# Reading lists ahead and reordering the rounds of a fused attention and expert kernel

## The chip, the core and the metric

The kernel runs on one core of a Trainium2 chip. The metric is device time in microseconds (us). The engines are TensorE (PE, with its weight loads as PEld), VectorE (DVE), ScalarE (ACT), GpSimd (POOL), and SyncE (SP), which issues most transfers. Each engine works through its own instructions in order, and waits between engines are semaphores.

## The reference

Eight batches of 512 tokens with 256 features go through one block:

```python
x = x + tanh(g_xattn[0]) * xattn(layernorm(x), ctx, ctx, mask)   # 16 heads of 16, softmax
x = x + tanh(g_ffn[0]) * ffn(layernorm(x))

def ffn(x):                                   # x: 4096 tokens x 256
    logits = x @ router_w + router_b          # 8 experts
    probs = softmax(logits)
    top_w, top_idx = top_k(probs, 2)
    comb = sum(top_w[..., None] * one_hot(top_idx, 8), axis=1)
    for e in range(8):
        h = gelu(x @ expert_up[e].T)          # 1024 wide
        output += comb[:, e] * (h @ expert_down[e].T)
    return output
```

All of it is float32. The mask leaves no more than 128 neighbouring keys here, and the kernel's near path reads only these; of the experts it computes only the two that a token has chosen.

## The kernel before

**Rounds.** `attend_near` runs rounds b = -1 to 7. A round has four groups g of three steps n, and a place in it is written (g,n). In round b the kernel computes the attention of batch b and the score maxima of batch b+1. `weights_T` (L1051 on) makes `w_ps` on TensorE and the exponentials `n_pT` on ScalarE; `weigh` makes `n_av` on TensorE and `raw`, `inv`, `n_o`, `oT` on VectorE; `find_tops` makes `t_ps` on TensorE and `tops` on VectorE; `lower_tops` makes `top_ps` and `ql`.

`between(old, new, next_)` lays further steps into the places of a round. They belong to the batch before (old = b-1), to the batch that is attended two rounds later (new = b+2) and to the one after that (next_ = b+3):

- old: `project_out` (`proj_ps`, and `x` on VectorE), `keep_x` (`out<-x` on SyncE), the statistics (`look`: `st_f_a`, `mv_f_a`), `settle` (a chain of 12 small VectorE operations that makes `rstd_end` and `shift`), the scalings `xn_f` on ScalarE (`scale`, L275), `keep_rows` (`rows<-xn_f` on SyncE), two turns (`xnT_ps_f`, then `x2T` on ScalarE) and the router's `logits` (`route_ps`, `lgT`).
- new: `keys_values` (`kv_ps`), the scalings `xn_a`, two turns (`xnT_ps_a`, `n_xnT`), `keys_T` (`k_ps`, `k`), `keys_less` (`km`), the queries (`q_ps`, `q`) and `add_bias` (GpSimd adds `bo` to `x`, 128x1024).
- next_: its statistics, settled together with those of old.

One round later, `route` (L330) transposes the logits (`lg_ps`), adds the bias (`lg`) and chooses two experts a token with some fifteen small VectorE operations and one exponential on ScalarE (`pr`). `place` (L363) counts with two pairs of matmuls (`place_ps`) at which line of its expert's list a token stands; ScalarE copies `counts`, and GpSimd works out `place_i`. Four `enter` steps a batch (L398), of two indirect transfers each, write the entries into a table in memory. At three points (in rounds 4 and 7 and in the tail) a plan divides what the table holds into groups of 256 rows, each with its expert.

**Groups.** A group s of rows goes through `list_rows(s)` (SyncE reads its list, `listed<-table`), `load(s)` (`up` and `down` of its expert, 1 MB each, SyncE, three buffers each), `fetch(s)` (GpSimd gathers `xg<-rows`), `turn` (`x_ps`, `xT`), `ups` (`h_ps` on TensorE, `hT` by Gelu on ScalarE), `fetch_y` (`y<-out`), and `downs` (`o_ps`, `y`, and GpSimd's `out<-y`). Groups 0 to 3 lie in rounds 4 to 7 by the table `amid`; groups 4 to 31 make up the tail. There `compute(s)` issues the steps of a group, with the list of group s+4 and the load of group s+2 at its end, and after each step takes one from a queue that holds what is left of the last two batches.

**What orders the work.** The program order is what the loops write. Instructions under `keep_in_program_order` (the first of a batch's scalings, first statistics, `settle`, the matmuls of scores and weights, and others) keep their place on their engine; the scheduler may move others. PSUM has one buffer for `n_av` and `o_ps` (`ps_o`), two for `bank` tiles (`ps_g`: `kv_ps`, `lg_ps`, `xnT_ps`, `k_ps`, `q_ps`, `top_ps`, `place_ps`, `proj_ps`, `route_ps`) and five for `t_ps`, `w_ps` and `x_ps` (`ps_s`). So a `bank` tile that waits holds up those behind it, and TensorE with them.

Of the kernel before, what the change touches and what calls it, by code (L numbers as in the profile page):

```python
# [23 lines left out]
E, FF = 8, 1024  # L24
# [44 lines left out]
def flamingo_layer(ctx: ExitStack, tc: tile.TileContext, a: dict, out: bass.AP):  # L69
# [190 lines left out]
    def shared(p2, small, bank):  # L260
        def layernorms(jobs, pin=False, measured=None):


            said, looks, settle_all = measured or measure(small, [job[:2] for job in jobs], pin)
            settle = lambda pin=False: settle_all(pin)

            def own(k):
                b, which, dst = jobs[k]

                def scale(ts):  # L270
                    if ts[0] == 0:
                        said[k] = p2.tile([P, QT, D], F32, tag="xn", name=f"xn_{which}_{b}")
                    for t in ts:
                        at = k * QT + t
                        ins = nc.scalar.activation(  # L275
                            said[k][:, t, :], xs[b][:, t, :], AF.Identity,
                            bias=said["shift"][:, at : at + 1], scale=said["rstd"][:, at : at + 1],
                        )
                        if t == ts[0] and pin:
                            tc.keep_in_program_order(ins)  # L280

                def turn(c):
                    ps = bank(f"xnT_ps_{which}_{b}_{c}")
                    for t in range(QT):
                        nc.tensor.transpose(ps[:, t * P : (t + 1) * P], said[k][:, t, c * P : (c + 1) * P], ident)
                    nc.scalar.copy((dst() if callable(dst) else dst)[:, c, :], ps)  # L286

                return (
                    lambda: said[k], [lambda ts=ts: scale(ts) for ts in ((0, 1), (2, 3))],
                    [lambda c=c: turn(c) for c in range(DC)],  # L290
                )

            return looks, settle, [own(k) for k in range(len(jobs))]
# [7 lines left out]
        def finish(b):  # L301
# [28 lines left out]
            def route():  # L330
                ps = bank(f"lg_ps{b}")[:, :P]
                nc.tensor.transpose(ps, said["lgT"], ident)
                lg = t3("lg")
                nc.vector.tensor_tensor(
                    lg, ps.rearrange("p (t e) -> p t e", t=QT)[:, :, :E], over_t(rb), ALU.add
                )
                mx = t2("mx")
                nc.vector.tensor_reduce(mx, lg, AX.X, ALU.max)
                nc.vector.tensor_tensor(lg, lg, over_e(mx), ALU.subtract)
                pr = t3("pr")  # L340
                nc.scalar.activation(pr, lg, AF.Exp)
                sm = t2("sm")
                nc.vector.tensor_reduce(sm, pr, AX.X, ALU.add)
                rs = t2("rs")
                nc.vector.reciprocal(rs, sm)
                nc.vector.tensor_tensor(pr, pr, over_e(rs), ALU.mult)
                top = t3("top")
                idx = t3("idx", U32)
                for t in range(QT):
                    nc.vector.max(top[:, t, :], pr[:, t, :])  # L350
                    nc.vector.max_index(idx[:, t, :], top[:, t, :], pr[:, t, :])
                ix = t3("ix")
                nc.vector.tensor_copy(ix, idx)
                picks = small.tile([P, QT, 2, E], F32, tag="picks", name=f"picks{b}", bufs=2)
                nc.vector.tensor_tensor(
                    picks, iota.unsqueeze(1).unsqueeze(1).to_broadcast([P, QT, 2, E]),
                    ix[:, :, :2].unsqueeze(3).to_broadcast([P, QT, 2, E]), ALU.is_equal,
                )
                both = t3("both")
                nc.vector.tensor_tensor(both, picks[:, :, 0, :], picks[:, :, 1, :], ALU.add)  # L360
                said["top"], said["picks"], said["both"] = top, picks, both
# [40 lines left out]
                    )  # L402

            places = [place] + [lambda t=t: enter(t) for t in range(b * QT, (b + 1) * QT)]
            return x2T, keep_x, keep_rows, logits, route, places

        return layernorms, finish

# [220 lines left out]
    def experts(pool, seen, half_bank, bank, row_bank):  # L629
# [281 lines left out]
        def downs(s):  # L911
            return [lambda h=h: go_down(s, h) for h in range(halves(s))]

        def compute(s, end, first):

            steps = [lambda: fetch(s + 2)] if s + 2 < end else []
            if s > first:
                steps.append(lambda: fetch_y(s - 1))
            up = ups(s)
            last = downs(s - 1) if s > first else []  # L920
            if s + 1 < end and s >= ALONE:
                turned_next = turns(s + 1)
                for step in up:
                    steps += [step, *turned_next[:1]]
                    turned_next = turned_next[1:]
                steps += turned_next + last
            elif s + 1 < end:
                steps += up + [lambda: turn(s + 1)] + last
            else:

                steps += up[:2] + last + up[2:]
            if s + 4 < end:
                steps.append(lambda: list_rows(s + 4))
            if s + 2 < end:
                steps.append(lambda: load(s + 2))
            if s + 1 == end:
                steps += [lambda: fetch_y(s), *downs(s)]
            return steps
# [29 lines left out]
    def attend_near(att):  # L968
# [143 lines left out]
        def between(old, new, next_):  # L1112
# [7 lines left out]

            jobs = []
            if old is not None:
                x2T, keep_x, keep_rows, logits, route, place = finish(old)
                jobs.append((old, "f", x2T))
            if next_ is not None:
                xnT[next_] = None
# [3 lines left out]
            if new is not None:  # L1130
# [4 lines left out]
                if new == 1:  # L1135
                    put(1, 1, *turns)
                    put(2, 1, keys_T)
                    put(3, 1, queries[0])
                    put(3, 2, queries[1], keys_less)
                else:  # L1140
                    put(1, 1, *turns, keys_T)
                    put(3, 0, keys_less)
                    put(2, 0, queries[0])
                    put(2, 1, queries[1])
# [4 lines left out]
                if new > 1:  # L1149
                    put(3, 0, bias)  # L1150
            if next_ is not None:
                put(*((2, 2) if old is None else (0, 2)), looks[-1])
            if old is not None:
                rows_f, scales, turns = normal[old, "f"]
                put(0, 1, lambda: project_out(old, (0, 1)))
                put(1, 0, lambda: project_out(old, (2, 3)), keep_x)
                put(1, 1, looks[0])
            if jobs:
                put(*((3, 1) if old is None else (1, 2)), settle)
            if old is not None:  # L1160
                put(2, 0, *scales)
                put(2, 2, lambda: keep_rows(rows_f()))
                put(3, 0, *turns)
                put(3, 1, logits)
                place, *enter = place
                counts = [count for count, end in zip(plans, PARTS) if old + 1 == end]
                later.append((route, place, enter, counts))
            return plan


        def begin():
# [19 lines left out]
            (7, 1): downs(2) + [lambda: load(4), lambda: turn_rows(3)],  # L1191
            (7, 2): [lambda: fetch_y(3)] + ups(3),
            (7, 3): [lambda: list_rows(5), lambda: fetch(5)] + downs(3)
            + [lambda: load(5), lambda: turn_rows(4), lambda: list_rows(6), lambda: list_rows(7)],
        }
        DONE = 4


        xnT, later = {}, deque()
# [4 lines left out]
        for b in range(-1, B):  # L1204
# [10 lines left out]
            if b == 0:  # L1215
                plan[0, 0] += looks
                plan[0, 1].insert(0, settle)
            for route, place, enter, counts in behind_route:
                plan[0, 2].append(route)
                plan[1, 2].append(place)  # L1220
                if counts:
                    plan[1, 2] += enter + counts
                else:
                    for where, step in zip(((1, 2), (2, 0), (2, 1), (2, 2)), enter):
                        plan[where].append(step)
            for g in range(4):
                c, i = g // 2, g % 2
# [17 lines left out]
        weigh(*behind)  # L1245
        rest = [step for steps in between(B - 1, None, None).values() for step in steps]
        wait = lambda: None
        (route, place, enter, _), (route_last, last, enter_last, counts) = later
        mixed = [step for pair in zip(rest, [route, place, *enter] + [wait] * len(rest)) for step in pair]
        spread = [step for one in enter_last for step in (one, wait, wait)]  # L1250
        queue = deque([*mixed, route_last, last, *spread, *counts])
        for s in range(DONE, MAIN):
            for step in compute(s, MAIN, DONE):
                step()
                if queue:
                    queue.popleft()()
                    if not queue:
                        assert s < ALONE
                        heads.close()
                        open_wide()  # L1260
# [3 lines left out]
    def attend_anywhere(att):  # L1264
# [141 lines left out]
            )  # L1406

        def end(b):
            x2T, keep_x, keep_rows, logits, route, place = finish(b)
            (look,), settle, ((normal, scales, turns),) = layernorms([(b, "f", x2T)])  # L1410
            return [keep_x, look, settle, *scales, lambda: keep_rows(normal()), *turns, logits, route, *place]

        def scores(b, h, t):
            q, kT, _ = qkv[b]
# [176 lines left out]
```

## Time and profile before

| | |
|---|---|
| median of 15 runs | 814.06 us (811.56 to 816.89) |
| profiled execution | 814.41 us |
| its span, first to last instruction | 812.6 us |
| mean granted TensorE clock | 0.971 |
| rounds -1 and 0, with the preparation | 0 to 69.8 us |
| rounds 1, 2, 3, 4 (from one `kv_ps` to the next) | 31.0, 39.1, 41.0, 38.2 us |
| rounds 5 to 7 | 219 to about 350 us |
| tail | about 350 us to the end |

The profile's page gives each engine's busy time and its share of the span, and the span in 40 slices of 20.3 us, in which a digit is the busy share in tenths. PEclk is the clock that the throttle granted to TensorE, in tenths of full speed. A timeline gives a start, a duration, the engine, the line, the operation, output and inputs, and in brackets the idle time of the engine just before, with what ended it. "remote" there means that no instruction of the profile was found to end the wait. Busy times by stretches give, behind the stretch and its length, a busy time and a count for each engine.

### The profile page before, as it was taken

What the parts mean: (1) busy time and instruction counts of PE and PEld (TensorE: products, weight loads), DVE (VectorE), ACT (ScalarE), POOL (GpSimd) and SP (SyncE); (2) the same over time, 40 slices, a digit from 0 to 9 for tenths busy, and PEclk for the clock granted to TensorE, in tenths of its full rate; (3) what the DMA queues carried; (4) which work ended last, traced back from release to release, by engine and by line L of the source; (5) the groups of instructions that cost most, each with busy time, mean ns of one, the idle gap of its engine ahead of it and who ended that gap; (6) DMA issues with size and microseconds to landing.
All of it is one profiled execution on the core that took longest, in us unless ns stands there. A gap on an engine that the chain in (4) does not pass through costs nothing.

```text
span 812.6 us, 11155 instructions
## 1 busy us (share of the span) xinstructions
PE 753.8 (93%) x3898; PEld 542.1 (67%) x3898; DVE 409.1 (50%) x1315; ACT 254.8 (31%) x487; POOL 313.2 (39%) x420
## 2 busy tenths in 40 slices
PE   8999988878989989998899999999999999999992
PEld 3444443434465656767688888888788788878872
DVE  8887895858673564633262352525343433523300
ACT  4563735354644434243312111111211211121110
POOL 2021115152636251546573534444443443344331
PEclk9998997989999999999999999999999999999997
DMA  5700211000473330143738566665754754654310
GB/s 163 264 7 8 78 33 56 27 30 27 153 284 110 108 115 20 53 146 91 262 107 319 187 211 218 191 237 180 248 168 151 239 182 151 200 199 177 99 52 25
DMA packets 82728, 113.32 MB, mean 139 GB/s; under 512 B 16605, under 2 KB 67552, under 8 KB 82656
## 3 DMA queue, kind: packets, MB, share of 16 engines
q1 hardware_dynamic: 70000, 85.16, 31.4%
q0 software_dynamic: 11840, 26.76, 10.0%
q8 instruction: 35, 0.57, 0.3%
q10 hardware_dynamic: 816, 0.53, 0.2%
q14 instruction: 37, 0.30, 0.1%
HBM read 92.66 MB, written 20.28 MB: 139 GB/s over the span
## 4 chain that ended last, share of the span: by engine, by line
PE 44%; DMA 15%; issue 14%; DVE 12%; POOL 8%; ACT 4%; another core or an unknown queue 1%; POOLq 0%; DVEq 0%; SPq 0%; ACTq 0%
PE o_ps L892 13%; PE h_ps L874 11%; DMA out<-y,listed 8%; DMA y<-out,listed 5%; PE w_ps L1058 5%; PE t_ps L1028 3%; PE n_av L1076 3%; DVE tops L1033 3%; DVE xT L863 2%; PE kv_ps L539 2%; POOL out L898 2%; PE proj_ps L1097 2%; POOL y L826 2%; DMA xg<-rows,listed 2%; PE top_ps L1046 1%
## 5 line engine op out<-in xcount | busy, mean ns | idle before, releaser
L892 PE MATMUL o_ps<-down,hT 128*128 128x256 f32 x1088 | 243.3, 381 | 4.7 <-DVE y L895 4.7
L874 PE MATMUL h_ps<-xT,up 128*128 128x256 f32 (+1 forms) x1024 | 242.9, 393 | 3.2 <-DVE xT L851 2.3
L892 PEld LDWEIGHTS o_ps<-down,hT 128*128 128x128 f32 x1088 | 206.1, 191 | 40.8 <-DVE y L895 6.3
L874 PEld LDWEIGHTS h_ps<-xT,up 128*128 128x128 f32 x1024 | 193.2, 190 | 46.0 <-issue 4.9
L863 DVE STREAM_TRANSPOSE xT<-xg 32x128 f32<-32x128 f32 (+1 forms) x368 | 115.6, 314 | 181.4 <-DMA xg<-rows,listed 176.6
L878 ACT ACTIVATE hT<-h_ps 128x512 f32<-128x512 f32 (+1 forms) x144 | 81.9, 573 | 346.2 <-PE h_ps L874 306.1
L898 POOL DMA_INDIRECT out<-y,listed x68 | 68.5, 1008 | 144.2 <-DVE y L895 125.7
L826 POOL DMA_INDIRECT y<-out,listed x68 | 65.0, 956 | 81.6 <-DMA out<-y,listed 56.7
L1033 DVE TENSOR_REDUCE tops<-t_ps 128x4 f32<-128x512 f32 x128 | 79.4, 682 | 21.3 <-PE t_ps L1028 16.6
L1063 ACT ACTIVATE n_pT<-w_ps 128x512 f32<-128x512 f32 x128 | 67.8, 597 | 49.4 <-PE w_ps L1058 47.0
L826 POOL DMA_INDIRECT xg<-rows,listed x68 | 66.5, 978 | 37.8 <-issue 18.9
L398 POOL DMA_INDIRECT table<-entries,place_i x64 | 63.2, 988 | 24.4 <-issue 16.1
L895 DVE SCALAR_TENSOR_TENSOR y<-o_ps,listed,y 128x256 f32<-128x256 f32 x68 | 31.1, 481 | 73.1 <-PE o_ps L892 51.0
L1058 PE MATMUL w_ps<-ql,km 32*128 32x512 f32 x256 | 53.8, 691 | 1.8 <-DVE tops L1033 1.4
L1010 POOL TENSOR_TENSOR x<-x,bo 128x1024 f32<-128x1024 f32 x8 | 18.8, 2354 | 72.4 <-DVE bo L1009 42.4
L1082 DVE STREAM_TRANSPOSE raw<-n_av 128x512 f32<-128x512 f32 x32 | 22.8, 712 | 46.7 <-PE n_av L1076 20.6
L1028 PE MATMUL t_ps<-k,q 32*128 32x256 f32 x512 | 43.8, 408 | 1.2 <-ACT n_pT L1063 0.7
L1028 PEld LDWEIGHTS t_ps<-k,q 32*128 32x128 f32 x512 | 26.8, 184 | 22.4 <-issue 9.7
L1076 PE MATMUL n_av<-n_pT,nv 128*32 128x512 f32 x256 | 38.4, 675 | 1.1 <-DVE xT L851 1.1
L570 PE MATMUL q_ps<-n_xnT,wqT 128*128 128x512 f32 x64 | 31.4, 615 | 0.9 <-ACT n_xnT L286 0.6
L1097 PE MATMUL proj_ps<-woT,oT 128*128 128x256 f32 x128 | 31.5, 388 | 0.0
L391 POOL TENSOR_SCALAR entries<-top,tg 128x8 f32<-128x8 f32 x8 | 2.6, 325 | 70.3 <-DVE top L350 70.2
(220 smaller groups left out, 552.7 us busy)
## 6 DMA issues: line engine op xcount, KB each, us to landing
up<-in_upT SPq DMA_DIRECT2D x32, 1024.0 KB
down<-in_downT SPq DMA_DIRECT2D x32, 1024.0 KB
out<-x SPq DMA_DIRECT2D x8, 512.0 KB
rows<-xn_f SPq DMA_DIRECT2D x8, 512.0 KB
x<-in_x SPq DMA_DIRECT2D x7, 512.0 KB
table<-none SPq DMA_DIRECT2D x1, 2400.0 KB
xg<-rows,listed POOLq DMA_INDIRECT x68
y<-out,listed POOLq DMA_INDIRECT x68
```

Of the source, the lines that this page charges most:

```text
L398: nc.gpsimd.indirect_dma_start(out=table_parts[2 * t + i][:, :], out_offset=bass.IndirectOffsetOnAxis(ap=place_i[:, t, i : i + 1], axis=0) ...
L826: ins = nc.gpsimd.indirect_dma_start(out=dst, out_offset=None, in_=src[: seen[JOBS[s][0]], :], in_offset=bass.IndirectOffsetOnAxis(ap=list ...
L863: nc.vector.transpose(dst[32 * g : 32 * g + 32, i], src[32 * i : 32 * i + 32, g])
L874: nc.tensor.matmul(ps[:, i, :], lhsT=up[:, dc, (f + i) * P : (f + i + 1) * P], rhs=xT[:, dc, :], start=(dc == 0), stop=(dc == DC - 1),)
L878: nc.scalar.activation(made[s][:, f : f + m, :], ps, AF.Gelu)
L892: nc.tensor.matmul(ps, lhsT=hT[:, f, h * P : (h + 1) * P], rhs=down[:, f, :], start=(f == 0), stop=(f == FC - 1))
L898: ins = nc.gpsimd.indirect_dma_start(out=out_parts[h][:, :], out_offset=bass.IndirectOffsetOnAxis(ap=listed[:, n, h, 0:1], axis=0), in_=y[ ...
L1028: ins = nc.tensor.matmul(ps[j][:, u], lhsT=q[rows_j, c, t * P : (t + 1) * P], rhs=k[rows_j, c], start=True, stop=True)
L1033: nc.vector.tensor_reduce(top[:, 2 * tp : 2 * tp + 2, :].rearrange("p t (i x) -> p t i x", i=2)[:, :, :, 32 * j], ps[j], AX.X, ALU.max,)
L1058: ins = nc.tensor.matmul(ps[j], lhsT=km[rows_j, c, i, :], rhs=lowered[b, c][rows_j, i, :], start=True, stop=True)
L1063: nc.scalar.activation(pT[:, j, :], ps[j], AF.Exp)
L1076: ins = nc.tensor.matmul(av[32 * j : 32 * j + 32, :], lhsT=made_of(b)[3][:, 8 * c + 2 * j + r, :], rhs=pT[:, j, :], start=True, stop=True,)
```

## The change

1. **Lists.** In round 7, SyncE reads the lists of groups 6 to 16 together, behind the load of group 5 (before: 6 and 7 there, and the others in the tail, each behind the group four before it).
2. **Scalings.** All `xn_f` and `xn_a` scalings are pinned to their place in the program order, not only the first of a batch.
3. **Choice.** `route` is divided: `lg_ps` and `lg` go from (0,2) to (0,0), the choice of experts (`choose`, from `mx` to `both`) from (0,2) to (1,2), behind the statistics and `settle`, with its first operation pinned. In the rounds with a plan (4 and 7) both stay at (0,2).
4. **Place.** `place` goes from (1,2) to (2,2), and the table writes of a batch from (1,2), (2,0), (2,1), (2,2) to (2,2), (3,0), (3,1), (3,2), in the rounds without a plan.
5. **Keys.** `keys_T` goes from (1,1) to (1,2).
6. **The first round.** In rounds that have no old batch, the last statistics go from (2,2) to (1,2) and `settle` from (3,1) to (2,0).
7. **Queue of the tail.** The route and choice of a batch are one step, and the steps of the last but one are paired in the same order as before.

```diff
-                        if t == ts[0] and pin:
+                        if pin:
                             tc.keep_in_program_order(ins)
...
+            def choose():
+                lg = said["lg"]
                 mx = t2("mx")
-                nc.vector.tensor_reduce(mx, lg, AX.X, ALU.max)
+                tc.keep_in_program_order(nc.vector.tensor_reduce(mx, lg, AX.X, ALU.max))
...
-            if s + 4 < end:
+            if listed <= s + 4 < end:
                 steps.append(lambda: list_rows(s + 4))
...
-                    put(1, 1, *turns, keys_T)
+                    put(1, 1, *turns)
+                    put(1, 2, keys_T)
...
-                put(*((2, 2) if old is None else (0, 2)), looks[-1])
+                put(*((1, 2) if old is None else (0, 2)), looks[-1])
...
-                put(*((3, 1) if old is None else (1, 2)), settle)
+                put(*((2, 0) if old is None else (1, 2)), settle)
...
-            + [lambda: load(5), lambda: turn_rows(4), lambda: list_rows(6), lambda: list_rows(7)],
+            + [lambda: load(5), lambda: turn_rows(4), lambda: [list_rows(s) for s in range(6, LISTED)]],
         }
         DONE = 4
+        LISTED = SIZES[0] + SIZES[1]
...
-            for route, place, enter, counts in behind_route:
-                plan[0, 2].append(route)
-                plan[1, 2].append(place)
+            for route, choose, place, enter, counts in behind_route:
                 if counts:
-                    plan[1, 2] += enter + counts
+                    plan[0, 2] += [route, choose]
+                    plan[1, 2] += [place, *enter, *counts]
                 else:
-                    for where, step in zip(((1, 2), (2, 0), (2, 1), (2, 2)), enter):
+                    plan[0, 0].append(route)
+                    plan[1, 2].append(choose)
+                    for where, step in zip(((2, 2), (2, 2), (3, 0), (3, 1), (3, 2)), (place, *enter)):
                         plan[where].append(step)
...
-            for step in compute(s, MAIN, DONE):
+            for step in compute(s, MAIN, DONE, LISTED):
```

`LISTED` is 17: the first two plans have 5 and 12 groups.

More of the change, by code (lines that the diff above doesn't have):

```diff
@@ L332, in route @@
                 nc.tensor.transpose(ps, said["lgT"], ident)
[L333 removed]
+                said["lg"] = t3("lg")
                 nc.vector.tensor_tensor(
[L335 removed]
+                    said["lg"], ps.rearrange("p (t e) -> p t e", t=QT)[:, :, :E], over_t(rb), ALU.add
                 )
+            def choose():
+                lg = said["lg"]
                 mx = t2("mx")
[L338 removed]
+                tc.keep_in_program_order(nc.vector.tensor_reduce(mx, lg, AX.X, ALU.max))
                 nc.vector.tensor_tensor(lg, lg, over_e(mx), ALU.subtract)
@@ L404, in finish @@
             places = [place] + [lambda t=t: enter(t) for t in range(b * QT, (b + 1) * QT)]
-            return x2T, keep_x, keep_rows, logits, route, places
+            return x2T, keep_x, keep_rows, logits, route, choose, places
         return layernorms, finish
@@ L912, in downs, with compute @@
             return [lambda h=h: go_down(s, h) for h in range(halves(s))]
-        def compute(s, end, first):
+        def compute(s, end, first, listed=0):
             steps = [lambda: fetch(s + 2)] if s + 2 < end else []
@@ L1122, in between @@
             if old is not None:
-                x2T, keep_x, keep_rows, logits, route, place = finish(old)
+                x2T, keep_x, keep_rows, logits, route, choose, place = finish(old)
                 jobs.append((old, "f", x2T))
@@ L1166, in between @@
                 counts = [count for count, end in zip(plans, PARTS) if old + 1 == end]
-                later.append((route, place, enter, counts))
+                later.append((route, choose, place, enter, counts))
             return plan
@@ L1247, in attend_near, with choice @@
         wait = lambda: None
-        (route, place, enter, _), (route_last, last, enter_last, counts) = later
-        mixed = [step for pair in zip(rest, [route, place, *enter] + [wait] * len(rest)) for step in pair]
+        (route, choose, place, enter, _), (route_last, choose_last, last, enter_last, counts) = later
+        def choice(route, choose):
+            route()
+            choose()
+        first = [lambda: choice(route, choose), place, *enter]
+        mixed = [step for pair in zip(rest, first + [wait] * len(rest)) for step in pair]
         spread = [step for one in enter_last for step in (one, wait, wait)]
-        queue = deque([*mixed, route_last, last, *spread, *counts])
+        queue = deque([*mixed, lambda: choice(route_last, choose_last), last, *spread, *counts])
         for s in range(DONE, MAIN):
-            for step in compute(s, MAIN, DONE):
+            for step in compute(s, MAIN, DONE, LISTED):
                 step()
@@ L1408, in end @@
         def end(b):
-            x2T, keep_x, keep_rows, logits, route, place = finish(b)
+            x2T, keep_x, keep_rows, logits, route, choose, place = finish(b)
             (look,), settle, ((normal, scales, turns),) = layernorms([(b, "f", x2T)])
-            return [keep_x, look, settle, *scales, lambda: keep_rows(normal()), *turns, logits, route, *place]
+            return [keep_x, look, settle, *scales, lambda: keep_rows(normal()), *turns, logits, route, choose, *place]
         def scores(b, h, t):
```

## The prediction

> **What bounds the kernel now.** I read the page's busy shares and 40 slices first, for which engine is bound when.
>
> ```profile
> PE 753.8 (93%) x3898; PEld 542.1 (67%) x3898; DVE 409.1 (50%) x1315; ACT 254.8 (31%) x487; POOL 313.2 (39%) x420
> ...
> PE   8999988878989989998899999999999999999992
> ...
> DVE  8887895858673564633262352525343433523300
> ...
> PEclk9998997989999999999999999999999999999997
> ```
>
> Behind slice 20 TensorE is always at nine tenths: the tail of expert groups is bound by its matmuls, and only a wait of TensorE can be won there. In the rounds (slices 2 to 17) VectorE is near it in places. So I read next the timeline of TensorE over round 3; a bracket gives the idle time ahead of a row and what ended it.
>
> ```profile
> 147.96 0.33 PE L332 MATMUL lg_ps<-ident,lgT 128*128 128x128 f32 x1 [0.80 <-DVE x L1102]
> ...
> 155.13 0.66 PE L285 MATMUL xnT_ps_a<-ident,xn_a 128*128 128x128 f32 x4 [1.19 <-DVE x L1102]
> ...
> 157.87 0.41 PE L368 MATMUL place_ps<-both,before 128*128 128x32 f32 x2 [0.75 <-ACT k L557]
> ...
> 163.59 1.13 PE L1028 MATMUL t_ps<-k,q 32*128 32x256 f32 x10 [0.47 <-ACT n_pT L1063]
> ...
> 174.91 1.14 PE L323 MATMUL route_ps<-x2T,rw 128*32 128x128 f32 x16 [3.68 <-ACT x2T L286]
> ```
>
> TensorE waits some tenths of a us here and there and then 3.68 us. The busy times by stretches of this round (length, then TensorE, its weight loads, VectorE, ScalarE, GpSimd, clock, DMA share, GB/s) say where a wait counts.
>
> ```profile
> 144.80:167.90 23.10, 19.66 (x125) 10.53 (x125) 21.70 (x73) 11.74 (x26) 7.07 (x18) 1.00 0.12 39
> 167.90:174.50 6.60, 3.33 (x36) 1.74 (x32) 1.46 (x4) 3.29 (x8) 4.27 (x6) 1.00 0.12 38
> 174.50:181.30 6.80, 6.39 (x37) 2.23 (x38) 3.48 (x6) 3.17 (x7) 2.31 (x1) 0.50 0.02 4
> ```
>
> Up to 167.9 VectorE is busy 21.70 of 23.10 us: it is the bound, and TensorE's 23.10 - 19.66 = 3.44 us of waits are slack. Then comes a hole in which no engine is busy for two thirds, and then TensorE at half the granted clock. VectorE's and GpSimd's timelines show the hole's ends.
>
> ```profile
> 172.84 0.72 DVE L1082 STREAM_TRANSPOSE raw<-n_av 128x512 f32<-128x512 f32 x1 [4.99 <-remote]
> ```
>
> ```profile
> 171.73 0.96 POOL L398 DMA_INDIRECT table<-entries,place_i  x1 [0.30 <-issue]
> ```
>
> TensorE's `n_av` ran at 168.07 for 1.06 us, yet `raw`, its reader, starts at 172.84, just behind the last of the eight table writes (162.78 to 172.69). Round 6 has the same: `raw` at 305.27 after 3.69 idle, writes until 303.59. So completions of TensorE seem to be seen late there. The 512 KB `rows<-xn_f` is under way in the same time (issued 166.09, traffic over by 168.5). Round 1, with rows and no table writes, has no such hole; round 5, with both, none over 1 us.
>
> **Part 1, VectorE's order (rounds 2, 3, 5, 6).** `lg` moves to the round's start, the ten operations behind it (3.6 us, 150.20 to 153.80) from before the statistics to behind `settle`, the place matmuls from (1,2) to (2,2). Nothing is removed. VectorE's work in the stretch stays 21.7 us, so the most to win is its idle time, 1.40 us a round. The waits for `x` (0.80, 1.19) go, since `lg_ps` stands behind `kv_ps` and the four `xn_a` scalings (0.59 each on ScalarE) stand together a step earlier; what is late next is `both`: the place matmuls stand in TensorE's order ahead of the next `w_ps`, so `w_ps`, `n_av` and `t_ps` queue behind them, and `tops` on VectorE for those. I expect 3.44 - 0.7 = 2.7 us of TensorE's slack to collect there. Bounds: 0 to 1.40 won a round while VectorE stays the bound; I take the middle, 0.7, since two of four waits end in VectorE: 4 x 0.7 = **2.8 us**. Pinning the other scalings costs 0: ScalarE is busy 11.74 of 23.10.
>
> **Part 2, round 0.** The statistics and `settle` of batch 2 (58.46 to 62.50, 4.0 us) move a step or two earlier. Now they stand ahead of `tops` at 63.94, for which TensorE waits:
>
> ```profile
> 64.67 3.26 PE L1058 MATMUL w_ps<-ql,km 32*128 32x512 f32 x6 [1.44 <-DVE tops L1033]
> ```
>
> The wait goes: **1.4 us**. Half clock follows it (about 65.4 to 71.7); if that goes too, another 3.2; if VectorE is as late an earlier step on, 0 in all. Bounds 0 to 4.6; the row itself is the value.
>
> **Part 3, lists.** Eleven are issued together in round 7. One takes SyncE 0.38 us and two stand 0.63 apart: 6.9 us, on no compute engine. The load of group 6 stood behind list 8 (382.64) and goes ahead of it, so its cover is over 15 us. GpSimd's table writes lose two waits for a list (3.14 at 384.54, 1.26 at 421.91), with 20 us until what they feed is used. On TensorE one wait lay behind list 10, through `up` of group 8:
>
> ```profile
> 425.80 4.55 PE L874 MATMUL h_ps<-xT,up 128*128 128x256 f32 x20 [0.93 <-DMA up<-in_upT]
> ```
>
> It goes: **0.9 us**. Bounds: 0 (another transfer is late instead) to 3.1, GpSimd's longest wait. The other queues' moves (`out<-x` of batch 7 behind group 6's load, `rows` behind two lists) are 0: their readers are a batch or 30 us away.
>
> **Part 4, the table writes' place.** They go from beside `rows<-xn_f` to 8 to 10 us later, with GpSimd's `add_bias` (2.35) put ahead in rounds 2 and 3 and `out<-y` in 5 and 6. If the hole needs the writes alone, it moves with them and is worth 0; if it needs them beside the rows, it goes. TensorE's waits in it are 3.68 (round 3), 3.64 (6), 0.93 + 1.75 (2) and 0.93 (4): 10.9 us. Bounds 0 to 10.9. Its end falls with the last write, 4 us behind the rows' traffic, so I take 0.
>
> **Part 5, the activation tables.** In round 5 `pr` comes between two Gelus: two more loads of 1.28 us on ScalarE, 2.6 us. It waits 3.38 us for `h_ps` near there (235.13), which is the cover: 0; without it up to 2.6 lost. The Trainium skill, "ScalarE: Activation LUTs", section "What ACT_TABLE_LOAD costs", puts a switch at some 2.66 us, a drain of 1.38 with it. The trace shows a load from 243.98 to 245.26 and `n_pT` at 245.27, so no drain behind it; by the page two switches would be 5.3 us, more than the cover, and the sum 2 us worse.
>
> **Sum.** 2.8 + 1.4 + 0.9 = 5.1 us. The profiled execution took 814.41 (span 812.6, 1.8 outside of it) and stands 0.35 over the median of 814.06, so it can be used as it is: 814.4 - 5.1 = **809.3 us**.
>
> **Rivals.** *The hole goes (faster).* For it: rounds 2, 3, 4 and 6 have rows and writes together, round 1 rows alone and no hole. Against: round 5, and the hole's end. Half of the 10.9 us, since some wait for `raw` stays, gives 809.3 - 5.5 = **804 us**; all of it 798.4.
>
> *The collected wait slows the clock (slower).* Place: the place matmuls at (2,2), rounds 2, 3, 5, 6. Half clock follows waits of 3.68 and of 1.44 us (65.4); it doesn't follow 1.19. If it decides from some 1.44 us, the collected 2.7 us draw a stretch. The shortest seen last about 3.4 us (208.4 to 212, 348.5 to 351.9), so 1.7 lost each, and part 1's gain with it: 814.4 + 4 x 1.7 - 1.4 - 0.9 = **818.9 us**. Against: VectorE is the bound there and covers some of a slow TensorE; and 1.80 us at 226.79 drew none. The Trainium skill, "TensorE: Matmul & The Clock Gate", Part 1, says that the clock is halved after a whole idle window of some 3.4 us. The 3.67 us hole ahead of 174.5 agrees; the 1.44 us at 64.67, and 348.5, ahead of which no wait over 0.9 stands, do not. By the page this rival would cost nothing, by the row of 64.67 it costs 6.8.
>
> *Nothing moves.* The waits are all slack behind VectorE (part 1 at 0) and the others fall to what comes next: **814 us**.
>
> **How the numbers follow.** Forecast (807 to 812): 0.34. The hole goes: 0.24. Nothing moves: 0.10. Slower: 0.32. A measurement of this kernel tells about 0.2% (1.6 us) from no change. Faster is 0.34 + 0.24 = 0.58, same 0.10, slower 0.32; both signs hold much, so the forecast's own range stands above. The range reaches from 799, which leaves out only a full loss of the hole with more of parts 1 and 2, to 821, the slow rival with most of part 5's 2.6 us on top.
>
> **What would show it.** Part 1 right: no waits for `x` at `lg_ps` and `xnT_ps_a`, one of 2 to 3 us at the place matmuls, VectorE busy over 22 of 23 us. Part 2: no wait of `w_ps` near 64. Part 3: `up` of group 6 issued before 370, no wait at group 8. Part 4: `raw` in rounds 3 and 6 again after 3 us or more, ended with the last table write. Wrong, if half clock stands at the place matmuls (slower), or if `raw` follows `n_av` at once in those rounds (804).

## The result, and the profile after

The changed kernel takes 825.17 us (median of 11 runs, 820.04 to 828.82) where the kernel before takes 814.13 (56 runs, 810.15 to 818.32): 1.0138 times as long, 95% interval 1.0122 to 1.0155. The forecast was 809.3, its range 799 to 821. The profiled execution took 821.16 us, at a span of 819.4, some 4 us under the median; its span is 6.8 over that of before.

The page of the changed kernel, the same lines as for before:

```profile
PE 757.3 (92%) x3898; PEld 548.7 (67%) x3898; DVE 410.5 (50%) x1315; ACT 258.0 (31%) x489; POOL 313.3 (38%) x420
...
PE   8999999988898989999499999999999999999992
...
DVE  7888887758664375532134444534433423533300
...
PEclk9999999889898889999799999999999999999997
```

TensorE is busy 3.5 us longer (757.3 against 753.8), at a mean granted clock of 0.962 against 0.971, and the rest of the 6.8 us is waiting. Slice 20 (389 to 410 us, in the tail) has TensorE at four tenths, where before it stood at eight, and every slice behind it at nine. To see where the two part, a marker is wanted that both have in the same order. `n_av` is one: 32 groups, four a round. This table has, for the profiled executions, the lead (minus) or lag against before at the start of `n_av`:

| place | before, us | after | order alone (e2) | e5 | e12 |
|---|---|---|---|---|---|
| round 0, g3 | 67.9 | -2.7 | -3.3 | -3.0 | -3.3 |
| round 1, g3 | 99.7 | -4.7 | -5.3 | -5.0 | -5.3 |
| round 3, g1 | 159.5 | -13.9 | -15.9 | -12.6 | -14.9 |
| round 3, g3 | 179.0 | -13.1 | -16.8 | -15.3 | -17.5 |
| round 4, g0 | 188.6 | -8.0 | -14.0 | -9.3 | -18.6 |
| round 5, g3 | 267.6 | -9.2 | -13.8 | -6.7 | -19.2 |
| round 6, g0 | 280.9 | -1.0 | -5.6 | -7.2 | -16.1 |
| round 7, g3 | 361.1 | -2.1 | -7.1 | -8.8 | -24.1 |
| end of the span | 812.6 | +6.8 | -2.3 | -5.0 | -12.9 |

The profiled execution of e2 is the fastest of its six, 5.2 us under their median, so the last row of its column shows less than the order cost.

The change does win early: 13.9 us by round 3, more than was forecast. It gives 5 back at the end of round 3, 8 between the last group of round 5 and the first of round 6, and 9 in the tail. TensorE's timeline of the changed kernel has a wait at each of the last two places:

```profile
255.54 0.65 PE L323 MATMUL route_ps<-x2T,rw 128*32 128x128 f32 x16
...
263.09 0.47 PE L332 MATMUL lg_ps<-ident,lgT 128*128 128x128 f32 x1 [3.62 <-issue]
```

```profile
391.11 0.64 PE L323 MATMUL route_ps<-x2T,rw 128*32 128x128 f32 x16
391.69 3.72 PE L877 MATMUL h_ps<-xT,up 128*128 128x256 f32 x16
403.51 0.48 PE L332 MATMUL lg_ps<-ident,lgT 128*128 128x128 f32 x1 [8.11 <-ACT lgT L328]
```

`lg_ps` waits for `lgT`, ScalarE's copy of `route_ps`. ScalarE's timeline of the changed kernel at both places:

```profile
262.77 0.27 ACT L328 COPY lgT<-route_ps 128x128 f32<-128x128 f32 x1 [7.98 <-remote]
```

```profile
403.20 0.27 ACT L328 COPY lgT<-route_ps 128x128 f32<-128x128 f32 x1 [9.36 <-remote]
```

`route_ps` was through at 256.2 and 391.8, and `lgT` waits for nothing but TensorE; still it started 6.6 and 11.4 us later. So this is the hole of the prediction (a completion of TensorE that is seen late), moved and grown. I call it the **hold**. GpSimd's timeline at the two places has the last table write of round 5, and the fourteenth and last of a run of transfers in the tail (eight table writes, four gathers `xg`, two `out<-y`, without a pause since 383.20):

```profile
260.99 0.96 POOL L401 DMA_INDIRECT table<-entries,place_i  x1 [0.30 <-issue]
```

```profile
399.86 1.01 POOL L901 DMA_INDIRECT out<-y,listed  x1 [0.30 <-issue]
```

The hold ends 0.8 and 2.3 us behind them. The stretches behind the two waits run at half clock (columns as in the prediction):

```profile
263.00:272.00 9.00, 8.91 (x28) 6.72 (x29) 7.21 (x10) 3.98 (x7) 7.08 (x7) 0.50 0.17 51
...
395.40:403.50 8.10, 0.01 (x1) 0.00 (x0) 0.00 (x0) 0.27 (x1) 4.63 (x6) 0.67 0.28 90
403.50:412.00 8.50, 5.89 (x16) 4.61 (x17) 3.34 (x22) 2.71 (x4) 1.89 (x3) 0.51 0.11 32
```

From 395.4 to 403.2, where `lgT` starts, no compute engine but GpSimd does anything. The theory to be tested: **a run of GpSimd's indirect transfers without a pause holds TensorE's completions once it has lasted some 6 us, until about its end**; the changed order has the runs end where `lgT` is wanted at once, and the lists read ahead make one long run out of two in the tail. Rivals: the order costs by itself; the lists cost by themselves (other transfers collide); the late place matmuls cost by their own waits.

### The profile page after: what moved, and what is told of

Its sections match the earlier page's. It is cut to its first block, busy times and chain, and to the rows that moved or that the text cites. A ratio compares the mean times of both kernels' runs of the same rounds, so it can differ in the third digit from the quotient of the medians.

```text
span 819.4 us, 11154 instructions
## 1 busy us (share of the span) xinstructions
PE 757.3 (92%) x3898; PEld 548.7 (67%) x3898; DVE 410.5 (50%) x1315; ACT 258.0 (31%) x489; POOL 313.3 (38%) x420
## 5 line engine op out<-in xcount | busy, mean ns | idle before, releaser
L877 PE MATMUL h_ps<-xT,up 128*128 128x256 f32 (+1 forms) x1024 | 247.4, 399 | 4.2 <-DVE xT L854 2.6
L877 PEld LDWEIGHTS h_ps<-xT,up 128*128 128x128 f32 x1024 | 196.4, 193 | 48.9 <-issue 5.6
L1036 DVE TENSOR_REDUCE tops<-t_ps 128x4 f32<-128x512 f32 x128 | 79.4, 683 | 20.7 <-PE t_ps L1031 16.8
L1061 PE MATMUL w_ps<-ql,km 32*128 32x512 f32 x256 | 58.6, 673 | 0.2 <-DVE tops L1036 0.2
L1079 PE MATMUL n_av<-n_pT,nv 128*32 128x512 f32 x256 | 36.7, 647 | 2.8 <-DVE xT L854 2.7
L1061 PEld LDWEIGHTS w_ps<-ql,km 32*128 32x128 f32 x256 | 21.0, 190 | 14.9 <-DVE tops L1036 7.9
```

The source lines that it names most:

```text
L877: nc.tensor.matmul(ps[:, i, :], lhsT=up[:, dc, (f + i) * P : (f + i + 1) * P], rhs=xT[:, dc, :], start=(dc == 0), stop=(dc == DC - 1),)
L1036: nc.vector.tensor_reduce(top[:, 2 * tp : 2 * tp + 2, :].rearrange("p t (i x) -> p t i x", i=2)[:, :, :, 32 * j], ps[j], AX.X, ALU.max,)
L1061: ins = nc.tensor.matmul(ps[j], lhsT=km[rows_j, c, i, :], rhs=lowered[b, c][rows_j, i, :], start=True, stop=True)
L1079: ins = nc.tensor.matmul(av[32 * j : 32 * j + 32, :], lhsT=made_of(b)[3][:, 8 * c + 2 * j + r, :], rhs=pT[:, j, :], start=True, stop=True,)
```

## The experiments

Ratios are to the kernel before, run beside it on the same chip, with 95% intervals. The experiments went to five chips: e1 to e4 (before 811.6 us there), e5 to e8 (814.2), e9 to e12 (813.5), e13 to e16 (791.6), e17 and e18 (791.8). That the last two chips are 22 us faster with the same kernel is a finding, to which I come below.

**e1, the lists alone**, and **e2, the order alone.** e1 is before with

```diff
-            if s + 4 < end:
+            if listed <= s + 4 < end:
...
-            + [lambda: load(5), lambda: turn_rows(4), lambda: list_rows(6), lambda: list_rows(7)],
+            + [lambda: load(5), lambda: turn_rows(4), lambda: [list_rows(s) for s in range(6, LISTED)]],
```

and e2 is the changed kernel with these lines as before.

> The kernel before with the lists alone read ahead. Theory (a long run of indirect transfers issued by GpSimd without a pause holds back the completions that the other engines see of TensorE, and the list waits of the tail used to break this run): the run of eight table writes grows together with the gathers behind it, as in the changed kernel's 14 from 383 to 401 us, lgT waits some 9 us instead of 5.3, and the time is about 820 to 825. Rival (the moved order of the rounds is what costs): within 2 us of before, 812 to 815.

> The changed kernel with the lists read as before. Theory: the rounds keep their gain of some 3 us (the first long h_ps of the tail stood at 373.2 instead of 376.3) and the tail's run is broken by list waits again: 809 to 813. Rival (the order costs): 820 to 826.

e1: 816.69 us, 1.0065 (1.0047 to 1.0083). e2: 817.15 us, 1.0082 (1.0059 to 1.0104). Each half costs, and 0.65 + 0.82 is about the 1.38% of the whole. Both lie between the theory's figure and the rival's: neither half is harmless. In e1's profile `lgT` waits 8.63 us in the tail and `lg_ps` behind it 6.86, 4.5 more than before:

```profile
397.80 0.27 ACT L328 COPY lgT<-route_ps 128x128 f32<-128x128 f32 x1 [8.63 <-remote]
```

In e2's the order wins 16.8 us by round 3, and `lgT` waits 7.18 us in round 5 until 257.45, when the last table write has just been issued (256.44 to 257.40):

```profile
257.45 0.27 ACT L328 COPY lgT<-route_ps 128x128 f32<-128x128 f32 x1 [7.18 <-remote]
```

**e3 and e4, spaced writes.** The changed kernel with a multiplication on GpSimd that nothing needs, ahead of each table write of the last two batches (e3) or of all (e4):

```diff
             def enter(t):
                 for i in range(2):
+                    if b >= B - 2:      # e4: True
+                        tc.keep_in_program_order(nc.gpsimd.tensor_tensor(bv, bv, bv, ALU.mult))
                     nc.gpsimd.indirect_dma_start(
```

> The changed kernel with one idle GpSimd multiplication of 128x256 (some 0.7 us) ahead of each table write of the last two batches. Theory: the run is no longer without a pause, lgT's wait of 9.4 us falls to under 5, time 813 to 818. Rival (the transfers themselves collide, rows and weights beside the table writes): the wait stays 8 to 10 us or grows with the later end of the writes, time 824 to 829. If the hold lasts until the last write has landed whatever the pace, the wait grows by some 5 us: 829 or more.

> As e3, in all batches. Theory: the waits of 8.4 us (lgT, round 3), 3.6 (x2T, round 4) and 8.0 (lgT, round 5) fall too, 2 to 6 us under e3. Rival (hold until the last write has landed): the writes end 6 us later in each of six rounds, so 5 to 20 us over e3.

e3: 823.84 us, 1.0157 (1.0126 to 1.0189). e4: 826.03, 1.0170 (1.0146 to 1.0194). Neither is faster, against the theory's numbers. The profiles say why, in part: in e3 the wait at `lg_ps` in the tail is gone (TensorE has no wait over 0.9 us from 371 to 410), but GpSimd is some 5 us later in each batch, and `o_ps` waits for `y`, 3.15 us from 410 on and 8.81 from 427. In e4 ScalarE's waits of 8.4 us in round 3 and 3.6 in round 4 are down to 1.2 and 0.2, the 8.0 us in round 5 to 3.5, and TensorE waits 4.69 us for `xg` from 214 on and 3.3 and 3.0 at the starts of rounds 3 and 4. So in part spacing takes the hold away, and GpSimd's lateness costs as much, where the writes stand late already. It is no full test: only the multiplications were pinned, and in rounds 2, 3 and 5 of e4 seven of the eight writes still stand in one run (255.52 to 264.10 in round 5), with the other multiplications behind it.

**e5 to e7, where the order costs.** e5 is e2, and e6 the changed kernel, with rounds 5 and 6 as before; e7 is the changed kernel with `lg_ps` alone put back in these rounds:

```diff
                 if counts:
...
+                elif b > 4:                                   # e5, e6
+                    plan[0, 2] += [route, choose]
+                    for where, step in zip(((1, 2), (1, 2), (2, 0), (2, 1), (2, 2)), (place, *enter)):
+                        plan[where].append(step)
                 else:
-                    plan[0, 0].append(route)
+                    plan[0, 2 if b > 4 else 0].append(route)  # e7
```

> As e2 (order alone, lists as before), but rounds 5 and 6 keep route, choice, place and table writes where they were before. In e2 n_av was 13.8 us ahead of before at (5,3) and 5.6 ahead at (6,0): lgT waited 7.2 us for route_ps until the last table write was out, lg_ps at (0,0) waited for lgT, and half clock followed. Theory (the late writes hold back route_ps's completion just where lg_ps at (0,0) needs it): the lead stays over 11 us into round 7, and the time is 6 to 9 us under e2, 808 to 811. Rival (the lead is lost to later load, whatever the place): within 2 us of e2, 815 to 819.

> The changed kernel with rounds 5 and 6 as before. Theory: 6 to 9 us under the changed kernel's 822 to 825, 814 to 818, with the tail's 8.1 us wait at lg_ps still there. Rival: 822 to 826.

> The changed kernel with lg_ps alone back at (0,2) in rounds 5 and 6; choice, place and writes stay late. Theory as in e5, if lg_ps is the link: TensorE passes on to t_ps, h_ps and proj_ps while lgT is held, the 3.6 us wait at lg_ps and its half clock go, 4 to 7 us under the changed kernel, 816 to 820. Rival (the late place matmuls cost, or another instruction waits in lg_ps's stead): 822 to 826.

e5: 810.47 us, 0.9956 (0.9927 to 0.9984), faster than before. e6: 818.95, 1.0043 (1.0015 to 1.0071). e7: 825.39, 1.0108 (1.0061 to 1.0155). So the place of the choice and the writes in rounds 5 and 6 costs about 1% (0.95 by e6, 1.26 by e5), more than the order costs in all, and the lead lost there (8.2 us in e2) does not go in e5. But `lg_ps` is not the link: that part of the theory fell. e7's timelines show what took its place. ScalarE first:

```profile
265.63 0.27 ACT L328 COPY lgT<-route_ps 128x128 f32<-128x128 f32 x1 [7.28 <-remote]
267.17 2.07 ACT L1066 ACTIVATE n_pT<-w_ps 128x512 f32<-128x512 f32 x4 [1.27 <-remote]
```

Then TensorE:

```profile
267.82 2.62 PE L1031 MATMUL t_ps<-k,q 32*128 32x256 f32 x13 [4.17 <-ACT n_pT L1066]
```

`lgT` is at the head of ScalarE's queue, `n_pT` stands behind it, and `t_ps` waits for the buffers that `n_pT` empties. Whichever instruction waits for a held completion, its whole engine waits.

**e8, one pause in the tail.** e6 with three such multiplications between the fourth and fifth write of batch 6:

```diff
+                    if b == B - 2 and t % QT == 2 and i == 0:
+                        for _ in range(3):
+                            tc.keep_in_program_order(nc.gpsimd.tensor_tensor(bv, bv, bv, ALU.mult))
```

> As e6 with three idle GpSimd multiplications (0.62 us each) between the fourth and the fifth table write of batch 6 in the tail. Theory (it is the run without a pause that holds completions): the wait at lg_ps falls from 8 to under 5 us, 2 to 5 us under e6. Rival (one pause is too little, only spacing each write helps): same as e6 within 1.5 us.

819.35 us, 1.0050 (1.0024 to 1.0077), as e6. It tells nothing: the writes themselves were not pinned, and GpSimd's timeline has the three multiplications at 375.66, ahead of the whole batch, and the 14 transfers from 382.45 still in one run.

**e9, without writes**, and **e10, spaced writes in before.** e9 leaves out the table writes of batches 1, 2, 4 and 5, so the experts' part of these batches is missing (one constant of the table's empty lines is changed with it, from `TOKENS - 1` to 0). e10 is before with the multiplication of e4 for batches 0 to 5 (rounds 2 to 7), the writes pinned too.

```diff
-                for i in range(2):
+                for i in range(2 if b in (0, 3, 6, 7) else 0):     # e9
...
+                    if b < B - 2:                                  # e10
+                        tc.keep_in_program_order(nc.gpsimd.tensor_tensor(bv, bv, bv, ALU.mult))
-                    nc.gpsimd.indirect_dma_start(
+                    ins = nc.gpsimd.indirect_dma_start(
...
+                    tc.keep_in_program_order(ins)
```

> The kernel before without the table writes of batches 1, 2, 4 and 5 (rounds 3, 4, 6 and 7), whose rows so get no expert's part; rounds 2 and 5 keep theirs. Theory (the writes hold TensorE's completions): in rounds 3 and 6 raw follows n_av at once instead of after 4.99 and 3.69 us, in round 2 route_ps waits as before, and the start of the tail comes 8 to 15 us earlier. Rival (rows, or something else at the round's end, holds them): the waits stay.

> The kernel before with one idle GpSimd multiplication (0.62 us) ahead of each table write of batches 0 to 5, order fixed. Theory (a run of writes without a pause holds completions from its sixth microsecond on; spaced writes don't): the waits of raw in rounds 3 and 6 fall under 1 us, 3 to 8 us faster, 806 to 811. Rival (each write holds, or the hold lasts until the last write is out): as before or 2 to 8 us slower, since the writes end 5 us later.

e9: 0.9883 (0.9854 to 0.9913) by three executions of 802.62 to 807.65 us; the profile is of a fourth, of 814.67 us, and only the places of its waits are read. e10: 806.53, 0.9904 (0.9882 to 0.9925). This settles that the run of writes is behind the hold of the rounds. In e9, `raw` follows `n_av` at once in rounds 3 and 6; round 2, which has its writes, still has its waits at `route_ps`, and round 5, which has them too, its 4.97 us at `raw` (252.90). Round 4 has no writes in e9 and still one hold of 4.2 us on `lgT`, beside a run of six gathers (199.2 to 206.7): it need not be table writes. e10 does all the work of before and more, and is 1% faster. VectorE in round 3 of e10, to set beside the line at 172.84 in the prediction:

```profile
168.57 0.72 DVE L1086 STREAM_TRANSPOSE raw<-n_av 128x512 f32<-128x512 f32 x1 [0.99 <-PE n_av L1080]
```

GpSimd at the same time, at the pace of all writes of batches 0 to 5 in e10:

```profile
166.65 0.62 POOL L400 TENSOR_TENSOR bv<-bv 128x256 f32<-128x256 f32 x1
167.44 1.01 POOL L401 DMA_INDIRECT table<-entries,place_i  x1 [0.17 <-issue]
168.48 0.62 POOL L400 TENSOR_TENSOR bv<-bv 128x256 f32<-128x256 f32 x1
169.27 1.01 POOL L401 DMA_INDIRECT table<-entries,place_i  x1 [0.16 <-issue]
```

Writes go on before and after, `n_av` (167.44 to 168.50) is seen at once, and 4.99 us of idle time have become 0.99.

**e11 and e12, the order of rounds 2 and 3 without the hold.** e11 is e5 with the spacing of e10, e12 is e5 with one pause of four multiplications (2.7 us) between the fourth and fifth write, pinned (`t % QT == 2 and i == 0`).

> As e5 (order of rounds 2 and 3, lists as before) with the same spacing. Theory: 2 to 6 us under e5, 804 to 808. Rival: 811 to 817.

> As e5 with one pause of four such multiplications (2.5 us) between the fourth and fifth write of batches 0 to 5, order fixed. Theory (the length of the run without a pause decides): as e11 or up to 3 us better, since the writes end only 2.5 us later. Rival (the pace of the writes decides, not a single pause): the holds of 4 to 6 us stay, time as e5 or 1 to 4 us slower.

e11: 805.30 us, 0.9882 (0.9858 to 0.9906). e12: 800.66, 0.9831 (0.9809 to 0.9853). One pause does most of it, and delays GpSimd less. In the rounds of e10 and e11 `lgT` starts at most 0.65 us behind the end of `route_ps`; e12 still has one hold, in round 4, where `route_ps` ended at 194.80 and the last write was out at 197.22:

```profile
198.15 0.27 ACT L328 COPY lgT<-route_ps 128x128 f32<-128x128 f32 x1 [4.00 <-PE w_ps L1065]
```

The lead at the end of round 7 is 24.1 us; the tail gives 11 of it back, and has 13 us of waits for `up` in two places, the first of which is

```profile
370.73 1.22 PE L881 MATMUL h_ps<-xT,up 128*128 128x256 f32 x2 [6.78 <-DMA up<-in_upT]
```

Here `up` stands on SyncE behind a list, which waits for the table writes: what the lists ahead are good for shows only when the rounds are fast.

**e13 to e16, lists ahead with pauses.** e13 is e12 with the lists ahead; e14 was to have the pause also in the writes of batch 6 in the tail; e15 and e16 are the changed kernel (rounds 5 and 6 late) with the pauses of e13 and e14.

> As e12 (rounds 5 and 6 as before, a pause of 2.5 us between the fourth and fifth write of batches 0 to 5), but with the lists read ahead. Theory (in the tail the lists ahead take away the waits for up, 6.8 and 6.3 us in e12, and bring the run of 14 transfers with a hold of 7 to 10 us): within 4 us of e12, 798 to 805. Rival (lists ahead cost by themselves, whatever the hold): 806 to 810.

> As e13 with the same pause also in the writes of batch 6 in the tail, which splits the run of 14 into 4 and 10. Theory (the run holds): the wait at lg_ps in the tail is shorter by 3 us or more, 2 to 6 us under e13, 794 to 800. Rival (the tail's wait comes from something else): as e13 or 1 to 3 us over it.

> The changed kernel with the pause in the writes of batches 0 to 5 and nothing else. Theory (the late place in rounds 5 and 6 costs only through the hold): the 8 us lost from (5,3) to (6,0) shrink to under 3, and the time is within 3 us of e13, 799 to 806. Rival (the late place costs by itself): 5 to 9 us over e13, 805 to 812.

> The changed kernel with the pause in the writes of batches 0 to 6. Theory: as e15 less what e14 wins over e13, 796 to 803. Rival: as e15.

| | us | ratio to before (791.6) | interval |
|---|---|---|---|
| e13 | 787.26 | 0.9945 | 0.9926 to 0.9963 |
| e14 | 790.37 | 0.9990 | 0.9976 to 1.0004 |
| e15 | 792.05 | 0.9998 | 0.9984 to 1.0012 |
| e16 | 795.88 | 1.0064 | 1.0042 to 1.0085 |

Before takes 791.6 us on this chip, so the expected times in us are void, and the comparisons on this chip stand. e14 and e16 tell nothing of a pause inside the tail's run, since it isn't there. GpSimd's timeline of e14 has the four multiplications ahead of the whole batch, and behind them the 14 transfers in one run, from 363.65 to 381.27 (in e16 the same, 362.49 and 369.88 on):

```profile
356.26 2.69 POOL L403 TENSOR_TENSOR bv<-bv 128x256 f32<-128x256 f32 x4
...
363.65 1.06 POOL L404 DMA_INDIRECT table<-entries,place_i  x1 [0.86 <-POOL place_i L397]
```

They are 3 to 4 us slower with those 2.7 us of GpSimd's time: in part, `o_ps` waits 4.71 and 4.91 us for `y` (391.83 in e14, 398.08 in e16), where e13 and e15 have 2.74 and 1.91. The late place in rounds 5 and 6 costs 4.8 us (e15 over e13) also where no hold is seen: in e15 the place matmuls of round 6 wait 2.82 us for `both`, and the lead falls by 4.1 us there. And the run of 14 in e13's tail (364.3 to 382.0) holds nothing.

**e17 and e18, the chip.** The changed kernel itself and e13's, again.

> The changed kernel. If before is near 792 on this chip (no hold): theory 788 to 794, within 0.5% of before, as e15. If before is near 813 (hold): 822 to 826, as first measured. Rival (the change costs by itself): over 797 also where before is near 792.

> e13's kernel. Without the hold: 785 to 789 as there. With it: theory (the tail's run of 14 still holds, the waits for up are gone) 797 to 806, ratio to before 0.980 to 0.992; rival (lists ahead cost by themselves) over 808.

On another chip of this kind (before 791.76), the changed kernel takes 792.66 us, 1.0017 (1.0003 to 1.0030), and e18 787.94, 0.9949 (0.9935 to 0.9963). The same program, instruction by instruction, that lost 1.38% loses 0.17% here. Its timelines at the two places, to be set beside those of the result: ScalarE in round 5, where `route_ps` ended at 243.48, and TensorE's `lg_ps`,

```profile
243.55 0.27 ACT L328 COPY lgT<-route_ps 128x128 f32<-128x128 f32 x1 [1.46 <-PE route_ps L323]
```

```profile
246.69 0.33 PE L332 MATMUL lg_ps<-ident,lgT 128*128 128x128 f32 x1
```

with the eight writes of the batch going on from 239.34 to 249.24; and ScalarE in the tail, in the midst of a run of 14 (362.9 to 380.5):

```profile
369.92 0.27 ACT L328 COPY lgT<-route_ps 128x128 f32<-128x128 f32 x1
```

No wait at all, where the slower chip had 9.36 us. In the six profiles of these two chips (e13 to e18) all 48 `lgT` start within 0.13 us of the end of `route_ps`. So the hold takes two things, a long run and a chip that does it.

## Why the prediction was wrong

The step that failed is **part 4**, "if the hole needs the writes alone, it moves with them and is worth 0". The mechanism was read rightly (it does move with the writes, e9), and the bounds weren't: 0 to 10.9 us won, and no loss. Its signs misled too: `raw` does follow `n_av` at once where the hole of rounds 3 and 6 stood (159.13 and 305.48, each within 0.12 us of its end), which was named as the sign of 804 us. A wait that moves comes to lie beside something else. Before, the writes ended in the rounds' last group, beside `raw` and `x2T`. Eight us later they end beside `lgT`, which heads ScalarE's queue with `n_pT` behind it, in the round's first group. That cost 8 us in round 5 and some 5 in round 3. By e6 the late places of rounds 5 and 6 together make 0.95% (1.0138 to 1.0043), and by e15 about 0.6% of it is there without a hold, from the place matmuls' own wait.

One reading behind it was wrong as well. Round 5 of before was held to have rows and writes and no hole over 1 us, and stood as a point against the faster rival. That is so of TensorE alone, which had `o_ps` to do; VectorE's line of that round, after an `n_av` that ended at 255.92, has the hole like the others:

```profile
260.00 0.72 DVE L1082 STREAM_TRANSPOSE raw<-n_av 128x512 f32<-128x512 f32 x1 [5.00 <-PE xnT_ps_f L285]
```

**Part 3** failed for the same reason. The 0.9 us was looked for on TensorE and SyncE. That GpSimd's "two waits for a list" were pauses in a run of transfers, and that without them the run has 14, was in the numbers of the prediction; nothing of it was priced. It costs 0.65% alone (e1). The 0.9 us itself was right, and on a kernel with faster rounds it is 13 (e12's waits for `up`). On the chips without the hold I have no run of the lists alone.

**Part 1** was right in direction and too small: from the end of round 1 to the last group of round 3 the lead grows by 8.4 us in two rounds, where 0.7 a round was taken and 1.40 was the bound. Some of it is the hold that now falls elsewhere, since the bound counted only VectorE's stretch. The place matmuls do wait for `both`, 1.57, 1.75 and 2.82 us in rounds 2, 3 and 6, against 2.7 expected.

**Part 2**: the wait of 1.44 us at 64.67 is gone and so is the half clock behind it; the lead is 4.7 us at the end of round 1, the upper bound of 4.6 rather than the 1.4 taken. **Part 5** cost nothing that can be seen.

**The rivals.** The slower one named the right sign and a mechanism that exists: in e17, which has no hold, half clock stands from 118.7 behind the place matmuls' wait of 1.57 us, from 180.1 behind 1.60 and from 279.1 behind 2.81. It doesn't follow the 1.57 at 152.48:

```profile
118.70:125.50 6.80, 6.80 (x28) 3.19 (x28) 3.20 (x7) 4.03 (x8) 4.71 (x14) 0.50 0.26 84
153.00:156.40 3.40, 3.40 (x18) 1.21 (x18) 2.41 (x5) 2.38 (x6) 2.28 (x11) 1.00 0.19 68
180.20:183.60 3.40, 3.40 (x16) 0.40 (x12) 2.31 (x17) 1.72 (x5) 2.40 (x11) 0.51 0.00 0
279.20:285.90 6.70, 6.70 (x26) 3.35 (x23) 3.31 (x7) 3.01 (x6) 3.54 (x10) 0.50 0.22 73
```

But e17 is only 0.17% slower than before, so with its price the parts' gains about cancel; the 11 us aren't its work. The faster rival's cause, rows beside writes, falls with e10, in which both stand side by side without a hole.

The Trainium skill, "TensorE: Matmul & The Clock Gate", Part 1, was cited for a clock that is halved after a whole idle window of some 3.4 us. The rows of e17 differ: 1.57 us were enough once and not enough another time. The measurement decides, and a wait of 1.5 to 3 us among matmuls on 32 rows is to be counted as a risk. What else decides is open; the stretches of half clock in e17's rounds begin at 118.70, 180.14, 207.45 and 279.13, which lie whole multiples of 3.41 us apart, so where a wait falls may count beside its length.

What stays open: what in the chip holds the completions, and why two of five chips don't. That the kernel before is free of the hold on those two is argued from its 22 us and from e17, since no profile of it was taken there. The changed kernel with pauses (e15) was not run on a chip with the hold, so what the hold alone costs it there is argued from e17, and not measured by taking it away. Nor was e13's kernel, so no version is shown to be the best on both; e12 (0.9831 with the hold) and e13 (0.9945 without) beat both kernels where they ran.

## What to carry to other kernels

A stall that a change moves is priced at its new place, with all that is queued behind the instruction that will wait there; its bound is never zero on the side of loss. When a change removes waits from an engine, look at what they spaced: on the chips with the hold, a run of eight of GpSimd's indirect transfers was worth one pause of 2.7 us in its middle (e12 against e5), where nothing needed that time. And measure a difference of 1% on more than one chip, against the old kernel on the same one.

## What the runs showed of the hardware

- On three of the experiments' five chips, and in the two traces of the result, a run of indirect transfers issued by GpSimd every 1.27 us brings late completions of TensorE. By the semaphore updates in the trace, the last one on time comes 5.7 to 7.1 us after the run's start in the three runs read for it (168.51 for a run from 162.78 in before; 165.72 for one from 158.59 and 257.77 for one from 252.04 in the changed kernel), and the next when the run is issued or up to 2.3 us later. A hold can let some through in between: in before's run from 293.68 to 303.59 `ql` starts at 300.84, and `raw` is held until 305.27. With 0.6 us more from one transfer to the next it was not seen in the rounds (e10, e11); with 2.7 us once after four (e12), one of 3.4 us was left.
- The matmuls go on meanwhile as the records have them (`top_ps`, `w_ps` and `n_av` run behind a `route_ps` that nobody has seen end), so TensorE looks busy, and only its readers, most of them marked "remote", show the hold.
- The same kernel took 811.6 to 814.2 us on three chips and 791.6 and 791.8 on two.
